# Masking unchosen experts behind the relu on VectorE, not in PSUM, in a GNN and mixture-of-experts kernel

## The chip, the cores and the metric

The kernel runs on one core of one Trainium2 chip. The metric is the time of one execution on the device in microseconds, the median of several runs.

The core's engines run at the same time, each through its own instructions in order: TensorE (PE, with its weight loads shown as PEld), VectorE (DVE), ScalarE (ACT), GpSimd (POOL) and SyncE (SP), which here only issues DMAs. Each engine waits on semaphores for what others make. Matrix products accumulate in PSUM; everything else is in SBUF.

## The reference

Two layers over 6250 nodes with 256 features and 100000 edges. Each layer is a graph aggregation followed by a mixture of experts, with residual sums.

```python
x = x + gnn0(layernorm(x))      # segment_sum(w_e * (n @ Wl)[dst], src) + n @ Wr + biases
x = x + ffn0(layernorm(x))      # 8 experts, all applied, weighted by softmax
x = x + gnn1(layernorm(x))      # segment_sum(w_e * (n @ W)[src], dst) + bias
x = x + ffn1(layernorm(x))      # 32 experts, one chosen per node
```

The change touches the last line:

```python
logits = xf @ router_w.T + router_b
idx = argmax(logits, axis=-1)                             # one of 32 experts per node
h = relu(einsum('nd,ndh->nh', xf, W1[idx]) + b1[idx])     # D = 256, H = 64
out = relu(einsum('nh,nhd->nd', h, W2[idx]) + b2[idx])
```

## The kernel before, in words

The node features stay in SBUF as `X`, 49 tiles of 128 nodes. The kernel first sorts the edges by source for layer 0 (to about 400 us), then runs layer 0 (to about 1845 us), then layer 1.

**Layer 1's aggregation.** The edges lie in columns of 128, sorted by target. For each column POOL issues an indirect DMA that gathers 128 rows of `h1` into a tile `g` (L201, with 24 buffers), ACT multiplies by the edge weight (L230), DVE computes the rounding rest of that product (L231, a scalar_tensor_tensor with two SBUF inputs), and both halves make one tile `m` (12 buffers). DVE also makes one-hot matrices `s` of the targets, three columns at a time (L222). PE multiplies `s` and `m` into `acc` (L277). Eight columns later `acc` is copied and summed (L250, L251, L255, L262), transposed (L209), multiplied by the layer's weight (L214) and added to `X` (L215). The first 64 columns are gathered in layer 0 already ("early columns"; `early_columns` prepares their indices and weights).

**Layer 1's experts.** The nodes go in 13 blocks: 3 tiles, then 11 blocks of 4, then 2. `begin1` normalizes a block (L329 to L346, transposes at L340), computes the router's logits (L956), finds the expert of each node, makes a one-hot of it, repeated four times to fill 128 columns, and transposes this (L972) into `hotT`, which has expert numbers on partitions. It also makes `cold`, which is 1 where `hotT` is 0. All 32 experts are applied to all nodes: the hidden layer has 32 x 64 units, in 16 chunks of 128, two experts a chunk. `hidden1` makes one chunk for a block: two products with W1 (L983), a third product of `sel` and `cold` (L986), which adds -2^127 to the units of the experts that weren't chosen, and a relu with bias on ACT (L988), which turns these into 0. `outs1` multiplies the chunk by W2 and accumulates in `py` (L999); with the first chunk it also adds the chosen bias (L997). `end1` adds relu(py) to `X` (L1006) and writes it out. `sel` is made once, by DVE, at L1024, from an iota made at L119.

**The order.** The products of chunk c+1's hidden layer are written ahead of chunk c's `outs1`. Between them come columns of the next block's aggregation, spread by a plan (`aheads`, `Stream.upto`): in a block of four tiles, 64 columns over 32 places. `begin1` of the next block is called 5 chunks ahead of the end of a block. Each engine's instructions are put in order by the framework when the kernel is built; the order written is a priority, and the engine order can differ from it.

PSUM tiles that matter: `ph` has three buffers; `tr`, with one buffer, is shared by the transposes, the logits and `pg`.

Of the kernel before, what the change touches and what calls it, by code (L numbers as in the profile page):

```python
# [8 lines left out]
F32 = mybir.dt.float32  # L9
F32R = mybir.dt.float32r  # L10
BF = mybir.dt.bfloat16
I32 = mybir.dt.int32
AF = mybir.ActivationFunctionType
OP = mybir.AluOpType
AX = mybir.AxisListType

P = 128
# [5 lines left out]
NB = 4  # L23
# [11 lines left out]
NX1 = 32  # L35
H1 = 64
# [2 lines left out]
SJ = 3  # L39
LAG = 10  # L40
EARLY = 2
FAR = -2.0 ** 127
SRC_PAD = 8191
NEAR = 576
LN_EPS = 1e-5
# [4 lines left out]
def gnn_ffn_kernel(ctx: ExitStack, tc: tile.TileContext, a, out):  # L50
# [32 lines left out]
    nc = tc.nc  # L83

    const = ctx.enter_context(tc.tile_pool(name="const", bufs=1))
# [5 lines left out]
    h1 = dram.tile([NT * P, D], F32, name="h1")  # L91

    def across(name, pool=const):
# [14 lines left out]
    src_c = const.tile([P, NCOL], I32, name="src_c")  # L108
    val_c = const.tile([P, NCOL], F32, name="val_c")
# [5 lines left out]
    good1 = const.tile([P, 1], F32, name="good1")  # L115
    off = const.tile([P, 1], F32, name="off")

    which_x = const.tile([P, NX1], F32, name="which_x")
    nc.gpsimd.iota(which_x, pattern=[[1, NX1]], base=0, channel_multiplier=-1, allow_small_or_imprecise_dtypes=True)  # L119
    order = const.tile([P, NX1], F32, name="order")  # L120
    nc.gpsimd.iota(order, pattern=[[-1, NX1]], base=NX1, channel_multiplier=0, allow_small_or_imprecise_dtypes=True)
    edges_rec, edges_val = a["edges_rec"], a["edges_val"]
# [8 lines left out]
                   allow_small_or_imprecise_dtypes=True)  # L131
# [3 lines left out]
    psum = sort_ctx.enter_context(tc.tile_pool(name="psum0", bufs=1, space=bass.MemoryType.PSUM))  # L135
# [260 lines left out]
    def check_edges():  # L396
# [24 lines left out]
        for i in range(2):  # L421
# [9 lines left out]
                   allow_small_or_imprecise_dtypes=True)  # L431
    which_q = early.tile([P, P, 4], BF, name="which_q")
    nc.gpsimd.iota(which_q, pattern=[[1, P], [0, 4]], base=0, channel_multiplier=0,
                   allow_small_or_imprecise_dtypes=True)
# [3 lines left out]
                   allow_small_or_imprecise_dtypes=True)  # L438
# [180 lines left out]
    psum = dense_ctx.enter_context(tc.tile_pool(name="psum1", bufs=1, space=bass.MemoryType.PSUM))  # L619
# [12 lines left out]
    LIM = late[0] * P  # L632
    NE = EARLY * GC

    with tc.tile_pool(name="layer0", bufs=1) as wp, tc.tile_pool(name="outs0", bufs=1, side="right") as wo_pool, \
# [56 lines left out]
        def aggregate0():  # L692
            for b, tiles in enumerate(blocks0):
                idx, dl, w = edges[b]
                for i, t in enumerate(tiles):
                    acc = psum.tile([P, 2, D], F32, tag="agg", name="acc", bufs=2)
                    for j in range(EW):
                        if j % SJ == 0:
                            s = one_hots(wp, dl[:, i, :], j, 3)
                        m = weighted(wp, h0, idx[:, i, j:j + 1], w[:, i, j:j + 1], 12, 6)  # L700
                        nc.tensor.matmul(acc, s[:, j % SJ, :], m, start=(j == 0), stop=(j == EW - 1))  # L701
                        if j == EW - 1:
                            for half in range(2):
                                nc.vector.tensor_add(X[:, t, :], X[:, t, :], acc[:, half, :])
                        yield

            for _ in columns1(wp, psum, range(NE), h1[:LIM, :], idx_e, w_e, (3, 12, 6, 2)):
                yield
            while True:
                yield  # L710
# [84 lines left out]
        def load1(k, half):  # L795
# [4 lines left out]
            else:  # L800
                cs = slice(half * NC1 // 2, (half + 1) * NC1 // 2)
                x = a["L1_ffn_W2"].rearrange("e h d -> (e h) d").rearrange("(c p) d -> p c d", p=P)
                nc.sync.dma_start(w2f[:, cs, :], x[:, cs, :])


        idx_e = wp.tile([P, NE], I32, name="idx_e")
        w_e = wp.tile([P, NE], F32, name="w_e")

        def early_columns():
            nc.vector.tensor_scalar(w_e, src_c[:, :NE], float(LIM), None, op0=OP.is_lt)  # L810
            nc.vector.tensor_tensor(w_e, w_e, val_c[:, :NE], OP.mult)
            nc.vector.tensor_scalar(idx_e, src_c[:, :NE], float(LIM - 1), None, op0=OP.min)


        n_late = len(late)
# [74 lines left out]
        block = begin0(blocks0[0])  # L890
# [47 lines left out]

    with tc.tile_pool(name="layer1", bufs=1, reuse_waits="tile") as wp, \
            tc.tile_pool(name="psum_y1", bufs=1, space=bass.MemoryType.PSUM, reuse_waits="tile") as psum_y:  # L940

        sel_x = wp.tile([P, NX1, H1], BF, name="sel")
        sel = sel_x.rearrange("q (c s) i -> q c (s i)", s=2)
        nought = wp.tile([P, 2 * D], BF, name="nought")

        done = []
# [1 line left out]
        def begin1(pool, tiles):  # L948

            n = len(tiles)  # L950
            nw = n * P
            nT = norm_t(pool, psum, tiles)
            pl = psum.tile([P, NB, NX1], F32, tag="tr", name="pl", bufs=1)
            for j in range(n):
                for k in range(2):
                    nc.tensor.matmul(pl[:, j, :], nT[:, k, j * P:(j + 1) * P], rw[:, k, :],  # L956
                                     start=(k == 0), stop=(k == 1))
            hot = work.tile([P, NB, NX1], F32, tag="hot", name="hot")
            top = work.tile([P, NB], F32, tag="top", name="top")
            g, m = hot[:, :n, :], top[:, :n]  # L960
            nc.vector.tensor_tensor(g, pl[:, :n, :], br1[:, None, :].to_broadcast([P, n, NX1]), OP.add)
            nc.vector.tensor_reduce(m, g, AX.X, OP.max)
            nc.vector.tensor_tensor(g, g, m[:, :, None].to_broadcast([P, n, NX1]), OP.is_equal)

            nc.vector.tensor_tensor(g, g, order[:, None, :].to_broadcast([P, n, NX1]), OP.mult)
            nc.vector.tensor_reduce(m, g, AX.X, OP.max)
            nc.vector.tensor_tensor(g, g, m[:, :, None].to_broadcast([P, n, NX1]), OP.is_equal)
            hots = work.tile([P, NB, P // NX1, NX1], F32, tag="hots", name="hots", bufs=1)
            nc.scalar.activation(hots[:, :n], g[:, :, None, :].to_broadcast([P, n, P // NX1, NX1]), AF.Copy)
            pg = psum.tile([P, NB * P], F32, tag="tr", name="pg", bufs=1)  # L970
            for j in range(n):
                turned = nc.tensor.transpose(pg[:, j * P:(j + 1) * P], hots[:, j], ident)  # L972
            hotT = pool.tile([P, NB * P], BF, tag="hotT", name="hotT", bufs=2)
            done[:] = [turned, nc.scalar.activation(hotT[:, :nw], pg[:, :nw], AF.Copy)]
            cold = pool.tile([P, NB * P], BF, tag="cold", name="cold", bufs=2)
            done.append(nc.vector.tensor_scalar(cold[:, :nw], pg[:, :nw], 0.5, None, op0=OP.is_lt))
            return nT, hotT, cold, nw

        def hidden1(pool, block, c):
            nT, _, cold, nw = block  # L980
            ph = psum.tile([P, NB * P], F32, tag="mm", name="ph", bufs=3)
            for k in range(2):
                nc.tensor.matmul(ph[:, :nw], w1f[:, k, c * P:(c + 1) * P], nT[:, k, :nw],  # L983
                                 start=(k == 0), stop=False)

            nc.tensor.matmul(ph[:, :nw], sel[:, c, :], cold[:, :nw], start=False, stop=True)  # L986
            hm = pool.tile([P, NB * P], F32, tag="hm", name="hm", bufs=4)
            nc.scalar.activation(hm[:, :nw], ph[:, :nw], AF.Relu, bias=b1[:, c:c + 1])  # L988
            return hm

        def outs1(block, c, now, py, n):
# [22 lines left out]
        with tc.tile_pool(name="flow1", bufs=1, reuse_waits="tile") as flow:  # L1014

            sums = Stream(columns1(flow, psum, range(NE, NREAL), h1, src_c, val_c, (5, EW + 6, 12, 4)))
            cum = [0] + [min(CS * (2 * tiles[-1] + 2) + CS // 2, NREAL) + LAG - NE for tiles in blocks1[1:]]
            plans = aheads(cum, 2 * NC1, [4] + [8] * (len(blocks1) - 1))
            block = begin1(flow, blocks1[0])

            behind = ExitStack()
            for ins in done:
                behind.enter_context(tc.issue_after(ins.ins))
            nc.vector.tensor_scalar(sel_x, which_x[:, :, None].to_broadcast([P, NX1, H1]), 0.0, FAR,  # L1024
                                    op0=OP.is_equal, op1=OP.mult)
            nc.vector.memset(nought, 0.0)
            hm = hidden1(flow, block, 0)
            for b, tiles in enumerate(blocks1):
                n = len(tiles)
                last = b + 1 == len(blocks1)  # L1030
                py = psum_y.tile([P, NB, D], F32, tag="y", name="py", bufs=1)
                mine = block
                for c in range(NC1):
                    sums.upto(plans[b][2 * c])
                    now = hm
                    if c + 1 < NC1:
                        hm = hidden1(flow, block, c + 1)
                    elif not last:
                        block = after
                        hm = hidden1(flow, block, 0)  # L1040
                    sums.upto(plans[b][2 * c + 1])
                    if b == 0 and c == 3:
                        behind.close()
                    outs1(mine, c, now, py, n)

                    if c == NC1 - (3 if b == 0 else 5) and not last:
                        after = begin1(flow, blocks1[b + 1])
                end1(flow, tiles, py)
# [60 lines left out]
```

## Time and profile before

| What | Value |
|---|---|
| Median of 3 runs | 2913.34 us (2908.56 to 2917.24) |
| The profiled execution's own time | 2906.32 us |
| Its span, first to last instruction | 2904.5 us |
| Mean granted TensorE clock | 0.974 |
| Busy over the span: PE, PEld | 2685.0 us (92%), 1750.0 us (60%) |
| Busy over the span: DVE, ACT, POOL | 2017.1 (69%), 1626.5 (56%), 1921.2 us (66%) |
| First chunk of layer 1's experts, last gather, last product | about 1860, 2784.5, 2897 us |
| Third products of `hidden1` (L986), one for a full block of 4 tiles | 208; record of 0.38 us |

Durations are of one execution, 7.0 us below the median. The records of PE's products overlap, since they are pipelined: the time from one start to the next is what a product costs. A few records of products are missing. In a line of a group, the figures after the first bar are busy time and the mean of one in ns, after the second the idle time just before and what ended most of it. In a line of the timeline the first two figures are start and duration in us.

### The profile page before, as it was taken

Reading aid. Unit: us, or ns where it says so; the run is one execution under the profiler, and the core shown is the slowest. Engines: PE = TensorE matmul, PEld = TensorE weight load, DVE = VectorE, ACT = ScalarE, POOL = GpSimd, SP = SyncE. Lnnn points to the kernel's source line nnn. Section 1 sums busy time; section 2 is a strip of 40 time slices with the busy share of each in tenths; the row PEclk is TensorE's granted clock in tenths of the full one; section 3 lists DMA queues with packets and bytes.
Section 4 is the critical chain, followed back from the end, with each engine's and each line's share of the span. In section 5 each row is a group of like instructions: output and inputs, shape, how many; then the busy total and the mean of one; then the engine's idle time right before and its main releaser. Section 6 shows DMA issues by size and latency. Waiting matters only on the chain.

```text
span 2904.5 us, 36970 instructions
## 1 busy us (share of the span) xinstructions
PE 2685.0 (92%) x10276; PEld 1750.0 (60%) x10336; DVE 2017.1 (69%) x4917; ACT 1626.5 (56%) x3790; POOL 1921.2 (66%) x1932
## 2 busy tenths in 40 slices
PE   5888848889999999999999998779999999999998
PEld 2444427666566666666666665556666666666666
DVE  8999978788767767667666646566666666666630
ACT  6777837655555555555555545355555555555532
POOL 4666667777767666776675527577777777777720
PEclk9999969999999999999999998989999999999999
DMA  4000043333333333333332214333333333333310
GB/s 150 19 19 19 19 144 97 104 101 101 93 99 96 89 102 93 91 103 95 90 100 82 82 40 126 95 108 100 108 109 109 106 108 102 108 107 109 109 46 12
DMA packets 123140, 260.73 MB, mean 90 GB/s; under 512 B 32236, under 2 KB 68904, under 8 KB 122920
## 3 DMA queue, kind: packets, MB, share of 16 engines
q0 software_dynamic: 79872, 218.21, 26.5%
q1 hardware_dynamic: 31672, 32.42, 3.4%
q10 hardware_dynamic: 11376, 7.60, 0.8%
q8 instruction: 85, 1.39, 0.2%
q14 instruction: 135, 1.11, 0.1%
HBM read 238.87 MB, written 19.25 MB: 89 GB/s over the span
## 4 chain that ended last, share of the span: by engine, by line
PE 60%; DMA 10%; issue 6%; DVE 5%; ACT 3%; POOL 2%; another core or an unknown queue 0%; ACTq 0%; POOLq 0%; SPq 0%; DVEq 0%
PE ph L748 19%; PE py L760 10%; PE py L999 8%; PE ph L983 8%; PE acc L701 6%; DMA g<-h,src_c 5%; PE acc L277 4%; DMA g<-h,idx 3%; POOL g L201 2%; DVE m L231 2%; ACT m L230 2%; DMA g<-h,idx_e 1%; PE ph L214 1%; PE tr L340 1%; PE pl L720 1%
## 5 line engine op out<-in xcount | busy, mean ns | idle before, releaser
L201 POOL DMA_INDIRECT g<-h,idx x882 | 900.0, 1020 | 390.7 <-DVE m L231 171.5
L201 POOL DMA_INDIRECT g<-h,src_c x718 | 724.9, 1010 | 244.2 <-issue 110.8
L230 ACT ACTIVATE m<-g,w 128x256 fp32r<-128x256 f32 x882 | 393.9, 500 | 254.5 <-PE acc L701 130.7
L230 ACT ACTIVATE m<-g,val_c 128x256 fp32r<-128x256 f32 x718 | 349.8, 503 | 278.5 <-PE acc L277 133.2
L751 ACT ACTIVATE hT<-ph,shift,scale 128x512 f32<-128x512 f32 (+3 forms) x480 | 328.8, 696 | 313.4 <-PE ph L748 312.0
L231 DVE SCALAR_TENSOR_TENSOR m<-g,val_c,m 128x256 fp32r<-128x256 f32 x718 | 336.8, 482 | 213.0 <-ACT m L230 209.2
L231 DVE SCALAR_TENSOR_TENSOR m<-g,w,m 128x256 fp32r<-128x256 f32 x882 | 397.3, 476 | 44.4 <-ACT m L230 43.5
L748 PE MATMUL ph<-nT,w 128*128 128x512 f32 (+3 forms) x960 | 376.1, 527 | 25.0 <-ACT hT L751 24.9
L760 PE MATMUL py<-wo,hT 128*128 128x256 f32 x1568 | 379.7, 385 | 14.0 <-DVE X L762 11.4
L999 PE MATMUL py<-w,hm 128*128 128x256 f32 x1568 | 385.2, 384 | 2.0 <-ACT hm L988 1.9
L983 PE MATMUL ph<-nT,w 128*128 128x512 f32 (+2 forms) x832 | 377.2, 574 | 0.0
L701 PE MATMUL acc<-m,s 128*128 128x512 f32 x882 | 339.7, 488 | 37.1 <-DVE scale L657 24.7
L748 PE MATMUL ph<-hT,w 128*128 128x512 f32 (+3 forms) x960 | 369.9, 519 | 0.5 <-ACT hT L751 0.5
L760 PEld LDWEIGHTS py<-wo,hT 128*128 128x128 f32 x1568 | 293.2, 192 | 80.6 <-DVE X L762 28.0
L277 PE MATMUL acc<-m,s 128*128 128x512 f32 x782 | 335.4, 502 | 5.7 <-DVE m L231 5.4
L999 PEld LDWEIGHTS py<-w,hm 128*128 128x128 f32 x1568 | 290.9, 192 | 51.8 <-ACT hm L988 3.9
L222 DVE TENSOR_TENSOR s<-col,dl 128x384 fp32r<-128x384 f32 x294 | 161.3, 550 | 185.7 <-PE acc L701 183.5
L748 PEld LDWEIGHTS ph<-nT,w 128*128 128x128 f32 x960 | 176.9, 197 | 175.1 <-issue 119.6
L748 PEld LDWEIGHTS ph<-hT,w 128*128 128x128 f32 x960 | 175.7, 193 | 118.5 <-issue 89.1
L988 ACT ACTIVATE hm<-ph,b 128x512 f32<-128x512 f32 (+2 forms) x208 | 136.8, 659 | 194.7 <-PE ph L986 141.9
L701 PEld LDWEIGHTS acc<-m,s 128*128 128x128 f32 x882 | 169.2, 195 | 108.9 <-issue 50.1
L983 PEld LDWEIGHTS ph<-nT,w 128*128 128x128 f32 x832 | 158.0, 192 | 102.2 <-issue 81.8
(248 smaller groups left out, 3343.7 us busy)
## 6 DMA issues: line engine op xcount, KB each, us to landing
g<-h,idx POOLq DMA_INDIRECT x882, 2.8
g<-h,src_c POOLq DMA_INDIRECT x718, 2.8
h<-hs SPq DMA_DIRECT2D x25, 256.0 KB, 2.1
X<-in_x_dram SPq DMA_DIRECT2D x12, 512.0 KB, 9.4
out_dram<-o SPq DMA_DIRECT2D x11, 512.0 KB, 3.4
h<-hs SPq DMA_DIRECT2D x9, 512.0 KB, 3.1
w<-in_L_ffn_W_dram ACTq DMA_DIRECT2D x2, 2048.0 KB, 11.9
wo<-in_L_ffn_Wo_dram ACTq DMA_DIRECT2D x1, 2048.0 KB, 21.1
```

The lines of the kernel that those rows point to most:

```text
L201: nc.gpsimd.indirect_dma_start(out=g, out_offset=None, in_=h, in_offset=bass.IndirectOffsetOnAxis(ap=idx, axis=0))
L222: nc.vector.tensor_tensor(s[:, :n], col[:, None, :].to_broadcast([P, n, P]), dl[:, j:j + n, None].to_broadcast([P, n, P]), OP.is_equal)
L230: nc.scalar.activation(m[:, 0, :], g, AF.Copy, scale=w)
L231: nc.vector.scalar_tensor_tensor(m[:, 1, :], g, w, m[:, 0, :], op0=OP.mult, op1=OP.subtract)
L277: nc.tensor.matmul(acc, s[:, (j - js.start) % SJ, :], m, start=opens, stop=done)
L701: nc.tensor.matmul(acc, s[:, j % SJ, :], m, start=(j == 0), stop=(j == EW - 1))
L748: nc.tensor.matmul(ph[:, :nw], (w1, w2)[layer][:, e, k, m * P:(m + 1) * P], src[:, k, :nw], start=(k == 0), stop=(k == 1))
L751: nc.scalar.activation(hT[:, m, :nw], ph[:, :nw], AF.Relu, bias=shift[:, layer, c:c + 1], scale=scale[:, layer, c:c + 1])
L760: nc.tensor.matmul(py, hT[:, k, j * P:(j + 1) * P], wo[:, e, k, :], start=(k == 0), stop=(k == 1))
L983: nc.tensor.matmul(ph[:, :nw], w1f[:, k, c * P:(c + 1) * P], nT[:, k, :nw], start=(k == 0), stop=False)
L988: nc.scalar.activation(hm[:, :nw], ph[:, :nw], AF.Relu, bias=b1[:, c:c + 1])
L999: nc.tensor.matmul(py[:, j, :], now[:, cols], w2f[:, c, :], start=False, stop=(c == NC1 - 1), skip_group_check=True)
```

## The change

The third product of `hidden1` goes. Instead `begin1` makes, for each block, a tile `whose` on all 128 partitions. A product of a constant `to_expert` with `hotT` gives the number of each node's expert, less 1 in the upper half of the partitions (whose units are those of odd experts), and DVE copies this to bf16. Behind each relu, DVE compares `whose` with 2c and multiplies the chunk by the result, in place (`hm`, f32). So chunk c keeps a unit only where the node's expert is the unit's. `cold`, `sel` and the iota behind `sel` go. `to_expert` is made by POOL at the start (a memset and an iota). `early_columns` writes in place into `src_c` and `val_c` where it had its own tiles, with two DVE instructions where there were three.

```diff
@@ constants
-    which_x = const.tile([P, NX1], F32, name="which_x")
-    nc.gpsimd.iota(which_x, pattern=[[1, NX1]], base=0, channel_multiplier=-1, allow_small_or_imprecise_dtypes=True)
+    to_expert = const.tile([P, P], BF, name="to_expert")
+    nc.gpsimd.memset(to_expert, 0.0)
+    nc.gpsimd.iota(to_expert[:NX1, :].rearrange("q (s i) -> q s i", s=2), pattern=[[-1, 2], [0, H1]], base=0,
+                   channel_multiplier=1, allow_small_or_imprecise_dtypes=True)
@@ aggregate0
-            for _ in columns1(wp, psum, range(NE), h1[:LIM, :], idx_e, w_e, (3, 12, 6, 2)):
+            for _ in columns1(wp, psum, range(NE), h1[:LIM, :], src_c, val_c, (3, 12, 6, 2)):
@@ early_columns
-            nc.vector.tensor_scalar(w_e, src_c[:, :NE], float(LIM), None, op0=OP.is_lt)
-            nc.vector.tensor_tensor(w_e, w_e, val_c[:, :NE], OP.mult)
-            nc.vector.tensor_scalar(idx_e, src_c[:, :NE], float(LIM - 1), None, op0=OP.min)
+            nc.vector.scalar_tensor_tensor(val_c[:, :NE], src_c[:, :NE], float(LIM), val_c[:, :NE],
+                                           op0=OP.is_lt, op1=OP.mult)
+            nc.vector.tensor_scalar(src_c[:, :NE], src_c[:, :NE], float(LIM - 1), None, op0=OP.min)
@@ begin1
-            cold = pool.tile([P, NB * P], BF, tag="cold", name="cold", bufs=2)
-            done.append(nc.vector.tensor_scalar(cold[:, :nw], pg[:, :nw], 0.5, None, op0=OP.is_lt))
-            return nT, hotT, cold, nw
+            pe = psum.tile([P, NB * P], F32, tag="tr", name="pe", bufs=1)
+            nc.tensor.matmul(pe[:, :nw], to_expert, hotT[:, :nw], start=True, stop=True)
+            whose = pool.tile([P, NB * P], BF, tag="whose", name="whose", bufs=2)
+            done.append(nc.vector.tensor_copy(whose[:, :nw], pe[:, :nw]))
+            return nT, hotT, whose, nw
@@ hidden1
                 nc.tensor.matmul(ph[:, :nw], w1f[:, k, c * P:(c + 1) * P], nT[:, k, :nw],
-                                 start=(k == 0), stop=False)
-            nc.tensor.matmul(ph[:, :nw], sel[:, c, :], cold[:, :nw], start=False, stop=True)
+                                 start=(k == 0), stop=(k == 1))
             hm = pool.tile([P, NB * P], F32, tag="hm", name="hm", bufs=4)
             nc.scalar.activation(hm[:, :nw], ph[:, :nw], AF.Relu, bias=b1[:, c:c + 1])
+            nc.vector.scalar_tensor_tensor(hm[:, :nw], whose[:, :nw], 2.0 * c, hm[:, :nw],
+                                           op0=OP.is_equal, op1=OP.mult)
@@ layer 1
-        sel_x = wp.tile([P, NX1, H1], BF, name="sel")
-        sel = sel_x.rearrange("q (c s) i -> q c (s i)", s=2)
...
-            nc.vector.tensor_scalar(sel_x, which_x[:, :, None].to_broadcast([P, NX1, H1]), 0.0, FAR,
-                                    op0=OP.is_equal, op1=OP.mult)
```

More of the change, by code (lines that the diff above doesn't have):

```diff
@@ L41 @@
 EARLY = 2
-FAR = -2.0 ** 127
 SRC_PAD = 8191
@@ L803, in load1 @@
                 nc.sync.dma_start(w2f[:, cs, :], x[:, cs, :])
-        idx_e = wp.tile([P, NE], I32, name="idx_e")
-        w_e = wp.tile([P, NE], F32, name="w_e")
         def early_columns():
-            nc.vector.tensor_scalar(w_e, src_c[:, :NE], float(LIM), None, op0=OP.is_lt)
-            nc.vector.tensor_tensor(w_e, w_e, val_c[:, :NE], OP.mult)
-            nc.vector.tensor_scalar(idx_e, src_c[:, :NE], float(LIM - 1), None, op0=OP.min)
+            nc.vector.scalar_tensor_tensor(val_c[:, :NE], src_c[:, :NE], float(LIM), val_c[:, :NE],
+                                           op0=OP.is_lt, op1=OP.mult)
+            nc.vector.tensor_scalar(src_c[:, :NE], src_c[:, :NE], float(LIM - 1), None, op0=OP.min)
         n_late = len(late)
@@ L974, in begin1 @@
             done[:] = [turned, nc.scalar.activation(hotT[:, :nw], pg[:, :nw], AF.Copy)]
-            cold = pool.tile([P, NB * P], BF, tag="cold", name="cold", bufs=2)
-            done.append(nc.vector.tensor_scalar(cold[:, :nw], pg[:, :nw], 0.5, None, op0=OP.is_lt))
-            return nT, hotT, cold, nw
+            pe = psum.tile([P, NB * P], F32, tag="tr", name="pe", bufs=1)
[3 more added lines that the diff above has]
+            return nT, hotT, whose, nw
         def hidden1(pool, block, c):
-            nT, _, cold, nw = block
+            nT, _, whose, nw = block
             ph = psum.tile([P, NB * P], F32, tag="mm", name="ph", bufs=3)
```

## Prediction

> **What bounds the kernel now.** I read the page first, then busy times by stretch, then the timeline of POOL beside that of DVE, then the waits. The change sits in layer 1, from about 1860 us to the end. On the page:
>
> ```profile
> L201 POOL DMA_INDIRECT g<-h,src_c x718 | 724.9, 1010 | 244.2 <-issue 110.8
> L231 DVE SCALAR_TENSOR_TENSOR m<-g,val_c,m 128x256 fp32r<-128x256 f32 x718 | 336.8, 482 | 213.0 <-ACT m L230 209.2
> L988 ACT ACTIVATE hm<-ph,b 128x512 f32<-128x512 f32 (+2 forms) x208 | 136.8, 659 | 194.7 <-PE ph L986 141.9
> ```
>
> Busy time by stretch (length; PE, PEld, DVE, ACT, POOL):
>
> ```profile
> 1860.00:2785.00 925.00, 887.00 (x3462) 610.33 (x3515) 596.92 (x1430) 495.88 (x1083) 710.54 (x705) 0.99 0.36 106
> 2785.00:2905.00 120.00, 111.22 (x469) 79.67 (x474) 17.24 (x49) 27.98 (x55) 0.41 (x1) 0.98 0.04 14
> ```
>
> PE at 96% and POOL at 77% invite the reading that PE is the bound. The timeline of POOL (start, duration, idle before) corrects it:
>
> ```profile
> 2466.27 1.02 POOL L201 DMA_INDIRECT g<-h,src_c  x1 [0.30 <-issue]
> 2467.60 1.31 POOL L201 DMA_INDIRECT g<-h,src_c  x1 [0.30 <-issue]
> 2469.22 0.95 POOL L201 DMA_INDIRECT g<-h,src_c  x1 [0.30 <-DMA g<-h,src_c]
> ```
>
> The 0.30 us ahead of each gather is always 0.30, whatever releaser is named: it is POOL's own gap. The 692 gathers from 1870 to 2780 us start 1.315 us apart in the mean, 1.245 at least: 1.25 of their own and 65 ns of lengthening (45 us in all). POOL never waits for a buffer; it paces the stage until its last gather at 2784.5. PE is only just behind: a block of four tiles takes 84 us, 64 gathers x 1.31, and PE's own start-to-start times add up to 80.8. The rest shows here (us, times, longest), 2140 to 2726:
>
> ```profile
> ACT m L230 <- PE acc L277: 99.0, 93, 2.6
> ACT m L230 <- DMA g<-h,src_c: 42.5, 70, 1.3
> PE tr L340 <- DVE xn L346: 10.7, 6, 2.6
> ```
>
> ACT runs ahead and waits sometimes for PE to free an m, sometimes for a gather's landing. DVE executes in order behind gathered data, so `begin1`'s statistics come late and PE stops at its transposes, some 1.7 us a block. After 2785 there are no gathers; PE alone sets the end.
>
> The lengthening has a cause that the trace shows. DVE, same moments:
>
> ```profile
> 2467.53 0.56 DVE L222 TENSOR_TENSOR s<-col,dl_c 128x384 fp32r<-128x384 f32 x1 [0.39 <-PE acc L277]
> 2469.25 0.41 DVE L255 TENSOR_TENSOR sums<-sums 64x256 f32<-64x256 f32 x1
> ```
>
> The one-hot, with two SBUF inputs, starts before the gather of 2467.60 and ends 0.49 us into it; that gather takes 1.31 instead of 0.95. L255 starts just after the next gather's start, which stays at 0.95. Over all 692 the rule holds: a two-SBUF-input DVE instruction already running at a gather's start lengthens it by (its remaining time - 115 ns); any other leaves it at 0.945. L231 costs 26.7 us so (38 ns each), L222 13.7 (59 ns each).
>
> [...] in the trace a cold product at 2859.78 is followed by py at 2860.00, 0.22.
>
> **The change, part by part.**
>
> *PE, removed.* 208 cold products: 176 x 0.216 + 16 x 0.16 (three tiles) + 16 x 0.11 (two tiles) = 42.3 us. Added: 13 products `pe`, 2.7 us. Before 2785 this buys almost nothing, since POOL's gathers cover it; if that cover went, it would be 39.6 us. Only the tail counts: 4.4 chunks of block 10 x 0.216, 16 of block 11 x 0.216 and 16 of block 12 x 0.107 = 6.1 us. A PE that isn't the limit may also stand up to a chunk (4.8 us) further ahead at the last gather; 0 to 5, I take 2.
>
> *DVE, added.* A mask behind each relu, 128x512, f32 and bf16 in, both SBUF, immediate scalar. No row shows it[...]. DVE goes from 597 to about 722 of 925 us, 78%: not the bound. `whose` replaces `cold` at the same size (0.69 from PSUM), `sel`'s 1.41 us go.
>
> *What queues behind the mask.* DVE waits there for the relu, and behind stand L231, L222, the sums and `begin1`'s statistics. PE waits for those; but from 2100 us its aggregation product starts 11 us or more, in 99 cases of 100, after the DVE product it needs, and the gathers have 24 buffers at 1.3 us each. The statistics come up to 0.7 us later, and PE stops longer at its transposes: hidden by POOL's pace, 0 to 2 us, I take 0. `hm` is needed two products later (3.4 us on, 1.7 for two tiles), relu plus mask take 1.4 and 0.9: no stall, except for the last chunk, where PE already waits 0.16 us for the relu. There 0.45 us are added.
>
> *POOL, lengthened.* The mask has two SBUF inputs. At a random moment an instruction of d ns costs the gathers (d-145)^2/(2 x 1310): for L231 43 (seen 38), for L222 64 (seen 59), for a mask 113, with three tiles 65. Under the gathers lie 16 of three tiles, 144 + 12 of four: 18.6 us. But the moments needn't be random. When ACT waits for landings, its relu comes right behind an m (2440.02, then 2440.43), so a mask would run about 2441.1 to 2441.8, between the gathers of 2440.9 and 2442.2, and cost nothing. So 0 to 18.6; I take half, 9. For the same reason L231 hits less: while ACT was under 3 us behind its gather (195 gathers) the lengthening was 45 ns, at 3 to 6 us (356) 64 to 76. With PE lighter the first kind should grow from 28% to some 60%: about -9 ns x 692 = -6 us; bounds -14 and +5 (masks push products into starts). POOL ends 3 us later.
>
> *At nothing.* `to_expert`'s memset and iota: POOL then waits 9.4 us for a bias; without that cover 0.4. `early_columns` in place: 0.2 us of DVE fewer, at 393 us. `pe` waits for hotT: up to 0.7 a block, under POOL's pace; 0.5 in all in the tail. The slot `tr` is held longer by it, same cover. `sel` gone at 1856: POOL's stream is running since 1845, nothing gained. No DMA moves, and the queue of SP stays as it is.
>
> Sum: POOL +3, tail -6.1 + 0.45 + 0.5, PE's lead -2: **-4 us**. The profiled execution took 2906.3 (span 2904.5), 7.0 below the median of 2913.3; it would go to 2902, the median to **2909**. A measurement tells about 0.3% (8.7 us) from no change, so this is no change; its own range is 2905 to 2922.
>
> **The rivals.**
>
> *Masks hit at random (slower).* All 18.6 us, products pushed into starts +5, tail -5: +18, 2931. For it: DVE at 78% runs more in bursts, and the stretches where ACT lags show 64 to 76 ns. Against: a lighter PE puts ACT on the gathers' beat. It decides from 21 ns more per gather, 14 us, at which the tail no longer brings the sum under +0.3%.
>
> *Gathers on beat (faster).* 45 ns each instead of 65: -14; masks +3; tail -5 and lead -2: -18, 2895. For it: the stretches at 45 ns. Against: L222 waits for PE and keeps its 14 us.
>
> *PE is the bound (faster).* All 39.6 us of products go: 2874. For it the 96%. Against: no gather waits, and 1.25 us is their least; this needs most of the 45 us of lengthening to vanish as well.
>
> *The mask doesn't spare the product.* Excluded by the diff: `stop` moves to the second k and the product is gone.
>
> **How the numbers follow.** No change 0.38, masks at random 0.24, on beat 0.32, PE bound 0.06: faster 0.38, same 0.38, slower 0.24. From 2888 to 2931 leaves out the PE-bound case and about half of the slower one, under 2 in 10.
>
> **What would show it.** After the change: L986 gone, 208 masks at 0.69; gather spacing 1.315 within 0.02; last gather within 2775 to 2805; from it to the end 112 to 115 us instead of 120; PE waiting longer at L340. Gathers with gaps other than 0.30, or PE still without stalls at L340, would prove the reading of POOL wrong; a spacing over 1.335 the slower rival right, under 1.30 the faster one.

## The result, and the profile after

The kernel became slower: 2922.85 us against 2911.34 us, medians of 11 runs each, a ratio of 1.0037 [1.0028, 1.0046]. That is +11.5 us where -4 was forecast. It lies inside the widest stated range, 2888 to 2931 us, but above the 2905 to 2922 that was given to no change, and on the side to which I had given the smallest chance.

The two profiled executions (spans 2904.5 and 2918.5 us) can be cut at the same three points, read from the starts of the gathers and of the last `py` product:

| us | before | after | difference |
|---|---|---|---|
| First gather of layer 1's main stream | 1840.95 | 1841.54 | +0.6 |
| From it to the last gather | 943.51 | 963.20 | +19.7 |
| From the last gather to the last product | 112.32 | 105.76 | -6.6 |
| From the last product to the end | 7.77 | 8.00 | +0.2 |

So the tail gained what it should, and the gather stage lost three times as much. The groups of both kernels between 1846 us and the end of the gathers, with before's line first (after the first bar: busy us and the mean of one in ns):

```profile
L201 POOL DMA_INDIRECT g<-h,src_c x711 | 718.2, 1010 | 216.6 <-issue 108.5 <-DVE m L231 50.3 <-DVE s L222 17.1
```

```profile
L202 POOL DMA_INDIRECT g<-h,src_c x711 | 736.2, 1035 | 219.0 <-issue 79.1 <-DVE m L232 53.3 <-DMA g<-h,src_c 22.5
```

There are as many gathers with the same idle time ahead of them (0.30 us each), but each takes 25 ns more. The page of after counts 782 gathers in this group, because the 64 early ones now read `src_c` too; hence the comparison by window.

Busy time by stretch of the kernel after (length; PE, PEld, DVE, ACT, POOL):

```profile
1861.00:2805.00 944.00, 873.92 (x3360) 605.53 (x3359) 686.73 (x1607) 503.22 (x1088) 729.52 (x705) 0.97 0.35 104
2805.00:2919.00 114.00, 105.71 (x441) 77.54 (x439) 35.23 (x82) 27.68 (x54) 0.73 (x1) 0.97 0.05 15
```

PE fell from 96% to 93% of the first stretch, DVE stands at 73%, and the stretch is 19 us longer: no engine is full. The mask itself costs DVE what was forecast (tile `whose`; min/median/max in ns):

```profile
L986 DVE SCALAR_TENSOR_TENSOR hm<-whose,hm x208: 424/684/762, 1861.2 to 2909.3; 128x512 f32<-128x512 bf16 x88, 128x384 f32<-128x384 bf16 x8, 128x256 f32<-128x256 bf16 x8
```

The waits of 2140 to 2726 us (us, times, longest):

```profile
ACT m L231 <- DMA g<-h,src_c: 85.1, 128, 3.1
ACT m L231 <- PE acc L278: 72.4, 73, 2.0
PE tr L341 <- DVE xn L347: 26.4, 7, 5.0
```

ACT now waits for landings 128 times instead of 70, and PE stops at its transposes for 26.4 us instead of 10.7. That the gathers are slower isn't the reason: e3 and e4 below, whose gathers keep the pace of before, show the like (123 and 92 waits; 19.0 and 21.7 us). But ACT came much less close to the gathers than forecast. The part of the gathers whose product on ACT starts less than 3 us after the gather does grew from 30% (207 of 692) to 34% (237 of 694), where the forecast went from 28% to some 60%.

**How a mask lengthens one gather.** POOL, then DVE, in the kernel after (start, duration). The 0.945 us of an undisturbed gather and the 0.115 are those of the prediction's rule:

```profile
1988.00 1.28 POOL L202 DMA_INDIRECT g<-h,src_c  x1 [0.30 <-ACT sums L251]
```

```profile
1987.78 0.68 DVE L986 SCALAR_TENSOR_TENSOR hm<-whose,hm 128x512 f32<-128x512 bf16 x1
1988.38 0.41 DVE L216 TENSOR_TENSOR X<-X,ph 128x256 f32<-128x256 f32 x1
```

The mask is running when the gather starts, and ends 0.46 us into it. Less 0.115 that makes 0.345; the gather takes 1.28 where 0.945 is its own, 0.335 more. L216 follows at once, but one of its inputs is in PSUM, and it adds nothing.

**How it lengthens one that an add holds.** The same two views, elsewhere:

```profile
2368.86 2.27 POOL L202 DMA_INDIRECT g<-h,src_c  x1 [0.30 <-issue]
```

```profile
2368.83 0.41 DVE L256 TENSOR_TENSOR sums<-sums 64x256 f32<-64x256 f32 x1
2369.17 0.54 DVE L223 TENSOR_TENSOR s<-col,dl_c 128x384 fp32r<-128x384 f32 x1
2369.64 0.67 DVE L986 SCALAR_TENSOR_TENSOR hm<-whose,hm 128x512 f32<-128x512 bf16 x1
2370.24 0.40 DVE L216 TENSOR_TENSOR X<-X,ph 128x256 f32<-128x256 f32 x1
```

The add over 64 partitions ends at 2369.24. By the prediction's rule the gather would have been 0.27 us longer; it is 1.33 longer, which is the time to the end of the mask at 2370.31, less 0.115. So it was held through three instructions that followed each other without a gap; such an unbroken run is called a held run below. Of the gathers of this kernel that started in a two-input instruction with another right behind it, those in such an add were held in 12 cases of 13, those in any other in 1 of 160.

Summed over the stage, each gather's time over 0.945 us put down to the instruction, or the unbroken run of them, that was on DVE when it started:

| Lengthening of the gathers, us | before | after |
|---|---|---|
| Masks (L986 of after) alone | - | 17.2 (64 gathers) |
| A 64-partition add, held until a mask's end | - | 10.1 (11 gathers) |
| Rounding rest `m` (L231, L232 of after) | 21.3 | 15.6 |
| One-hot `s` (L222, L223 of after) | 13.3 | 15.1 |
| 64-partition adds alone | 2.7 | 1.3 |
| Other held runs | 6.1 | 1.2 |
| All of it, small ones included | 46.2 | 64.9 |

Of before's 6.1 us, 3.65 fall to one gather that was held from a one-hot to the end of the ninth instruction behind it, at 1882.37, less 0.115:

```profile
1878.60 4.59 POOL L201 DMA_INDIRECT g<-h,src_c  x1 [0.30 <-issue]
```

```profile
1878.12 0.54 DVE L222 TENSOR_TENSOR s<-col,dl_c 128x384 fp32r<-128x384 f32 x1
1881.90 0.47 DVE L231 SCALAR_TENSOR_TENSOR m<-g,val_c,m 128x256 fp32r<-128x256 f32 x1
```

### The profile page after: what moved, and what is told of

It reads as the page before. It is cut to its first block, busy times and chain, and to the rows that moved or that the text cites. A ratio compares the mean times of both kernels' runs of the same rounds, so it can differ in the third digit from the quotient of the medians.

```text
span 2918.5 us, 36818 instructions
## 1 busy us (share of the span) xinstructions
PE 2661.7 (91%) x10141; PEld 1741.3 (60%) x10141; DVE 2120.5 (73%) x5123; ACT 1633.6 (56%) x3790; POOL 1942.1 (67%) x1933
## 4 chain that ended last, share of the span: by engine, by line
PE 63%; DVE 14%; DMA 10%; issue 5%; ACT 5%; POOL 1%; ACTq 0%; POOLq 0%; DVEq 0%
PE ph L749 19%; PE py L761 10%; PE py L998 8%; PE ph L981 7%; DMA g<-h,src_c 7%; PE acc L702 5%; PE acc L278 4%; PE put L531 3%; DMA g<-h,idx 3%; DVE m L232 3%; ACT m L231 2%; DVE loads L528 1%; POOL g L202 1%; ACT loads L503 1%; PE ph L571 1%
## 5 line engine op out<-in xcount | busy, mean ns | idle before, releaser
L202 POOL DMA_INDIRECT g<-h,src_c x782 | 810.1, 1036 | 309.7 <-issue 91.2
L231 ACT ACTIVATE m<-g,val_c 128x256 fp32r<-128x256 f32 x782 | 381.7, 504 | 342.6 <-DMA g<-h,src_c 186.8
L231 ACT ACTIVATE m<-g,w 128x256 fp32r<-128x256 f32 x882 | 394.7, 500 | 258.1 <-PE acc L702 138.7
L232 DVE SCALAR_TENSOR_TENSOR m<-g,val_c,m 128x256 fp32r<-128x256 f32 x782 | 362.1, 480 | 156.6 <-ACT m L231 154.2
L232 DVE SCALAR_TENSOR_TENSOR m<-g,w,m 128x256 fp32r<-128x256 f32 x882 | 397.7, 476 | 42.9 <-ACT m L231 41.4
L998 PE MATMUL py<-w,hm 128*128 128x256 f32 x1568 | 394.4, 389 | 9.1 <-DVE hm L986 9.0
L761 PE MATMUL py<-wo,hT 128*128 128x256 f32 x1568 | 381.1, 386 | 17.2 <-DVE X L763 14.5
L278 PE MATMUL acc<-m,s 128*128 128x512 f32 x782 | 375.1, 550 | 8.6 <-DVE m L232 8.3
L702 PE MATMUL acc<-m,s 128*128 128x512 f32 x882 | 341.3, 490 | 36.8 <-DVE scale L658 24.6
L998 PEld LDWEIGHTS py<-w,hm 128*128 128x128 f32 x1568 | 297.1, 196 | 64.0 <-DVE hm L986 13.8
L223 DVE TENSOR_TENSOR s<-col,dl 128x384 fp32r<-128x384 f32 x294 | 161.4, 551 | 186.7 <-PE acc L702 184.5
```

Source lines behind the costliest of these rows:

```text
L202: nc.gpsimd.indirect_dma_start(out=g, out_offset=None, in_=h, in_offset=bass.IndirectOffsetOnAxis(ap=idx, axis=0))
L223: nc.vector.tensor_tensor(s[:, :n], col[:, None, :].to_broadcast([P, n, P]), dl[:, j:j + n, None].to_broadcast([P, n, P]), OP.is_equal)
L231: nc.scalar.activation(m[:, 0, :], g, AF.Copy, scale=w)
L232: nc.vector.scalar_tensor_tensor(m[:, 1, :], g, w, m[:, 0, :], op0=OP.mult, op1=OP.subtract)
L278: nc.tensor.matmul(acc, s[:, (j - js.start) % SJ, :], m, start=opens, stop=done)
L761: nc.tensor.matmul(py, hT[:, k, j * P:(j + 1) * P], wo[:, e, k, :], start=(k == 0), stop=(k == 1))
```

## Experiments

Theory: POOL's gathers pace the stage; the masks lengthen them because both of a mask's inputs are in SBUF, and because runs that begin with a 64-partition add and end in a mask hold them longer. Rivals: DVE is simply too busy, so that what queues behind a mask comes late (any operation of that length would do); or the loss lies in the other edits of the change. The expectations call the theory that of the port and the first rival that of the queue; the port is only a name there, no run shows one.

**A neutral operation of the mask's size in the kernel before**, once with both inputs in SBUF, once with one of them in PSUM. The product on PE stays in both.

```diff
             nc.scalar.activation(hm[:, :nw], ph[:, :nw], AF.Relu, bias=b1[:, c:c + 1])
+            # e1
+            nc.vector.scalar_tensor_tensor(hm[:, :nw], cold[:, :nw], 2.0, hm[:, :nw],
+                                           op0=OP.is_lt, op1=OP.mult)
+            # e2, in its place
+            nc.vector.scalar_tensor_tensor(hm[:, :nw], ph[:, :nw], 0.0, hm[:, :nw],
+                                           op0=OP.mult, op1=OP.max)
```

> The kernel before, with its third product kept, and behind each relu a DVE instruction of the mask's size and place with two SBUF inputs (cold < 2, times hm: it multiplies by 1). Port theory[...]: gather spacing goes from 1.315 to about 1.340 us, last gather some 18 us later, the part after the last gather as before plus 0.5: +18 us, 1.006 of before. Queue theory (the mask hurts as one more instruction in DVE's order that waits for the relu, so that products and statistics come late and PE stands): a similar rise here, +10 to +18 us, so this run alone doesn't tell; its pair with one PSUM input does.

> As the run with two SBUF inputs, but the added DVE instruction reads ph from PSUM and hm from SBUF (max of ph times 0 and hm: it leaves hm as it is), same size, same place, same wait for the relu. Port theory: spacing stays at 1.315 within 0.005, time within 3 us of before (0.999 to 1.001). Queue theory: the same rise as with two SBUF inputs, +10 us or more.

Measured: 1.0055 [1.0039, 1.0070] with two SBUF inputs, 0.9974 [0.9963, 0.9984] with one in PSUM (before: 2911.32 us). The added operations, by tile, e1 first; some records are missing:

```profile
L989 DVE SCALAR_TENSOR_TENSOR hm<-cold,hm x202: 424/688/768, 1859.9 to 2899.2; 128x512 f32<-128x512 bf16 x88, 128x384 f32<-128x384 bf16 x8, 128x256 f32<-128x256 bf16 x5
```

```profile
L989 DVE SCALAR_TENSOR_TENSOR hm<-ph,hm x208: 424/690/693, 1865.2 to 2895.4; 128x512 f32<-128x512 f32 x88, 128x384 f32<-128x384 f32 x8, 128x256 f32<-128x256 f32 x8
```

They take the same time on DVE, 0.688 and 0.690 us, at the same place. Groups of the gathers in a window of the same length, again e1 first:

```profile
L201 POOL DMA_INDIRECT g<-h,src_c x698 | 721.6, 1034 | 212.7 <-issue 82.0 <-DVE m L231 58.5 <-DVE s L222 15.2
```

```profile
L201 POOL DMA_INDIRECT g<-h,src_c x714 | 717.0, 1004 | 241.7 <-issue 89.8 <-DVE m L231 64.0 <-PE corr L878 23.3
```

1034 ns against 1004 ns for a gather, and 16 gathers fewer in the same 934 us. In e2 not one gather's lengthening falls to the added operation; in e1 16.6 us fall to it alone and 5.5 to held runs that end in it. So DVE's added time costs nothing at this place, and the second SBUF input makes the whole difference of 20.7 us between the two: the first rival doesn't explain the loss. By which mechanism the second input does it, no run shows. That e2 comes out even a little faster than before was not expected; the table at the end of this section shows where that lies.

**The kernel after with the mask replaced by e2's operation, and without it.** Both leave the masking out.

```diff
-            nc.vector.scalar_tensor_tensor(hm[:, :nw], whose[:, :nw], 2.0 * c, hm[:, :nw],
-                                           op0=OP.is_equal, op1=OP.mult)
+            # e3; e4 has nothing here
+            nc.vector.scalar_tensor_tensor(hm[:, :nw], ph[:, :nw], 0.0, hm[:, :nw],
+                                           op0=OP.mult, op1=OP.max)
```

> The changed kernel with the mask replaced by the DVE instruction that reads ph from PSUM and hm from SBUF and leaves hm as it is: the masking is left out, the DVE work, its place and its waits stay. Port theory: spacing 1.31 us, the part after the last gather 105.8 instead of 112.3 us, so 6 to 9 us faster than before: 0.997 to 0.998. Queue theory: as the changed kernel, 1.003 to 1.004.

> The changed kernel with the mask left out and nothing in its place (units of unchosen experts stay). Port theory: 0.997 to 0.998 of before, as with the PSUM input, spacing at or a little under 1.31. Queue theory: clearly faster than the run with the PSUM input, by 5 us or more. A theory that pe, whose or the changed order of the rest cost the time: still slower than before.

Measured: 0.9982 [0.9974, 0.9990] and 0.9949 [0.9937, 0.9961]. Without the mask the kernel is 12.8 us faster than before in the medians, so the other edits together lose nothing and the second rival is out. The gathers of e3 in their stage:

```profile
L202 POOL DMA_INDIRECT g<-h,src_c x709 | 718.2, 1013 | 216.8 <-issue 73.6 <-DVE m L232 61.5 <-DVE s L223 18.6
```

1013 ns where after has 1035. But the medians of e3 and e4 differ by 7.8 us. That is more than the theory of the port has room for, and it is the sign that was set for the queue (5 us or more). So the two pairs don't agree on what an operation with a PSUM input costs: -6.4 us in e2 against before, +7.8 in e3 against e4. The profiles put e3's part into the gathers (48.8 and 41.6 us of lengthening), by instructions that both kernels have. Whether the added operation moved these instructions onto the gathers, or the order of the program did, is open. The loss of the kernel after is larger: it stands 16.5 us above e3, which has the same DVE time.

**Masks in two halves; full-partition adds; masks only where there are no gathers.** Three kernels and a control.

```diff
@@ e5, e5b: after
-            nc.vector.scalar_tensor_tensor(hm[:, :nw], whose[:, :nw], 2.0 * c, hm[:, :nw],
-                                           op0=OP.is_equal, op1=OP.mult)
+            for at in (slice(0, nw // 2), slice(nw // 2, nw)):
+                nc.vector.scalar_tensor_tensor(hm[:, at], whose[:, at], 2.0 * c, hm[:, at],
+                                               op0=OP.is_equal, op1=OP.mult)
@@ e7, e7b: after; e8, e8b: before
-                nc.vector.tensor_add(s[low], s[low], halves[q - 1][low])
+                nc.vector.tensor_add(s, s, halves[q - 1])
...
-                nc.vector.tensor_add(halves[q - 1][high], halves[q - 1][high], s[high])
+                nc.vector.tensor_add(halves[q - 1], halves[q - 1], s)
@@ e6, e6b: before, its product kept for blocks 0 to 10; in 11 and 12 the mask; the change's other edits as in after
+BARE = NT - 6
...
+            if tiles[0] >= BARE:
...
+                return nT, hotT, whose, nw, True
```

> The changed kernel with each mask cut into two instructions of half the length (256 columns, about 0.42 us each, 1.3 times the DVE time of one of 0.69). Port theory, with each instruction costing the gathers (d-145)^2/(2 x 1310) ns: 2 x 28 to 29 = 57 ns a mask in place of 113, so the masks' own 17 us fall to about 9 us, and the last gather comes 6 to 10 us earlier than in the changed kernel: 0.9995 to 1.0015 of before. Queue theory or a theory of DVE's total work: 21 us more of DVE work and 416 instructions in place of 208 make it slower than the changed kernel, 1.004 or more.

> The kernel before for blocks 0 to 10, with sel, cold and the third product; blocks 11 and 12, which run when all gathers are done, take whose and the mask. Port theory: no mask lies under a gather, the part after the last gather falls from 112.3 to about 107.5 us: 4 to 5 us faster than before, 0.998 to 0.999, and faster than the changed kernel by 14 us or more. A theory that pe, whose or the mask are dear by themselves (in the tail too): 1.000 or more.

> The changed kernel with the two adds of 64 partitions (of the halves of a tile's sums) made over all 128 partitions; the sums that leave it aren't the reference's. In the trace of the changed kernel 11 gathers that met such an add were held until the end of the mask behind it, 10 us in all, while gathers that met other two-input instructions were held for that one alone. If an add of half the partitions[...]: those cases go, the lengthening falls from 65 to 55 to 58 us, 0.997 of the changed kernel, 1.000 to 1.002 of before. If it is their place in the order (back-to-back instructions that wait for nothing): the held cases stay, and so does the time, 1.003 to 1.004.

> The kernel before with the same two adds over 128 partitions (the sums aren't the reference's): the control. In its trace 2 gathers were held beyond an add, 2.4 us in all. Either theory: within 3 us of before, 0.999 to 1.001.

This first set told nothing on the question. The kernel before itself took 3281.98 us there, and its gathers no longer follow at 0.30 us. A line of POOL's timeline in e8:

```profile
2611.09 0.95 POOL L201 DMA_INDIRECT g<-h,src_c  x1 [3.58 <-DVE m L231]
```

POOL stood idle 150 to 202 us beyond its own gaps between the 718 gathers of the stage in these four (before, in its usual run: 4 us), so that its gathers were not the pace. The stage also began late there, at 2007 to 2031 us instead of 1841. The ratios were 0.9948 [0.9931, 0.9965] for e5, 0.9979 [0.9954, 1.0004] for e6, 0.9965 [0.9947, 0.9982] for e7 and 1.0000 [0.9970, 1.0029] for e8: there the mask in halves and with full adds came out ahead of the kernel before. This would fit a stage in which PE's spared time counts, but the kernel after itself has no run there. Why all was slower is open; in these four profiles no gather shows when it landed. The four were repeated later, on a chip of the same number (13, both times), and there before took 2909.48 us.

> e5 again on a usual chip: masks in two halves. Port theory: 0.9995 to 1.0015 of before, the masks' own lengthening 17 us down to about 9. Theory of DVE's total work or of its queue: 1.004 or more.

Measured: 1.0025 [1.0016, 1.0034], a little above the expected. A half takes 0.417 us, so DVE works 0.15 us more for each chunk, 1.22 times a whole mask:

```profile
L987 DVE SCALAR_TENSOR_TENSOR hm<-whose,hm x416: 281/417/496, 1861.3 to 2906.6; 128x256 f32<-128x256 bf16 x117, 128x192 f32<-128x192 bf16 x11, 128x128 f32<-128x128 bf16 x11
```

The masks' own lengthening fell from 17.2 to 8.7 us: more DVE time, half of that loss. In the time of the whole the gain is not clear: the interval touches that of the kernel after, 1.0028 to 1.0046. What didn't fall enough is the held part: 4.8 us still go to gathers that an add holds through both halves, and further runs, whose start is neither a mask nor an add over 64 partitions, hold more than in after (6 that start in an `m`).

> e7 again on a usual chip: the changed kernel with the two half-partition adds made over all 128 partitions (its sums aren't the reference's). If the half-partition add[...]: lengthening 55 to 58 us instead of 65, 1.000 to 1.002 of before. If it is their place in the order: 1.003 to 1.004.

> e8 again on a usual chip, the control: the kernel before with the two adds over 128 partitions (its sums aren't the reference's). Either theory: 0.999 to 1.001 of before.

Measured: 1.0012 [1.0004, 1.0020] for after with full adds, 0.9984 [0.9974, 0.9995] for the control. In e7b no gather is held through a run. The same moment as above, POOL and then DVE:

```profile
2367.27 1.19 POOL L202 DMA_INDIRECT g<-h,src_c  x1 [0.30 <-issue]
2368.76 0.94 POOL L202 DMA_INDIRECT g<-h,src_c  x1 [0.30 <-DVE hm L986]
```

```profile
2367.22 0.42 DVE L256 TENSOR_TENSOR sums<-sums 128x256 f32<-128x256 f32 x1
2367.55 0.55 DVE L223 TENSOR_TENSOR s<-col,dl_c 128x384 fp32r<-128x384 f32 x1
2368.02 0.68 DVE L986 SCALAR_TENSOR_TENSOR hm<-whose,hm 128x512 f32<-128x512 bf16 x1
```

Again a gather starts just after the add, and the same three follow without a gap. But it is 0.245 us longer, the add's remaining 0.37 less 0.115, and lets the rest go by. In all 13 gathers of e7b started in an add with another two-input instruction right behind, and none was held. The masks alone lengthen by 14.2 us instead of 17.2, and the whole is 53.7 us instead of 64.9. The control's is 50.9 in its profiled execution, no less than before's 46.2: before has few such runs to lose. But its median came out 2.8 us lower where no change was expected, so of the 7.5 us between after and e7b some 5 are left to the held runs by the medians. That they are gone is shown by the trace.

> The same kernel as e6 again, for a chip on which the kernel before takes its usual 2911 us (e6 met a chip where it took 3282, with POOL idle for 238 us between gathers, so that nothing was paced by the gathers). Mask in the tail alone: 4 to 5 us faster than before, 0.998 to 0.999, gather spacing as before, 1.31 us, the part after the last gather about 107.5 us. If pe, whose or the mask are dear by themselves: 1.000 or more.

Measured: 0.9985 [0.9976, 0.9993], 2903.91 us. Busy by stretch:

```profile
2784.00:2899.00 115.00, 106.60 (x442) 77.82 (x444) 34.41 (x81) 28.02 (x55) 0.28 (x1) 0.98 0.04 14
```

Its last gather starts at 2783.33 (before: 2784.46), and from there to the last product it takes 107.6 us instead of 112.3. It keeps most of the tail's gain without the stage's loss and is the version that beats both kernels here, by 0.15% over before. That is no more than the control e8b gained, so its place in the tail is shown by its trace rather than by the median.

**All runs in one table**, one profiled execution each (us; the difference of medians is to before in the same set):

| Kernel | First to last gather | Lengthening in it | Difference of the two | Last gather to last product | Median, difference |
|---|---|---|---|---|---|
| before | 943.5 | 46.2 | 897.3 | 112.3 | 0 |
| after | 963.2 | 64.9 | 898.3 | 105.8 | +11.5 |
| e1, two SBUF inputs added | 960.5 | 63.2 | 897.3 | 111.2 | +14.3 |
| e2, PSUM input added | 940.0 | 42.9 | 897.1 | 111.2 | -6.4 |
| e3, after with PSUM input | 945.6 | 48.8 | 896.8 | 105.7 | -5.0 |
| e4, after without mask | 938.4 | 41.6 | 896.8 | 106.2 | -12.8 |
| e5b, after in halves | 957.2 | 60.4 | 896.8 | 107.1 | +8.2 |
| e7b, after with full adds | 950.6 | 53.7 | 896.9 | 107.8 | +4.0 |
| e8b, before with full adds | 948.1 | 50.9 | 897.2 | 112.0 | -2.8 |
| e6b, masks in the tail only | 942.7 | 46.6 | 896.1 | 107.6 | -5.6 |

The fourth column is 896.1 to 898.3 in all ten: POOL's gaps don't grow, and whatever PE, DVE and ACT have to do, the stage is the gathers' own time plus their lengthening. With the last-but-one column this gives the differences of the medians within 2 us, e8b excepted, whose profiled execution took 6.1 us more than its median. It leaves out where the stage begins, between 1839.8 and 1845.4 us in these executions. What the table leaves open is the lengthening of the kernels that have no masks under the gathers: 41.6 to 50.9 us, by the same instructions at other moments. In several of them one early gather alone, at 1876 to 1881 us, takes part of it by a held run: 3.65 us in before and in e4, 4.5 in e6b. This scatter between programs, of up to 0.3%, is as large as e2's and e8b's gains and the difference of e3 and e4; none of those is explained. The 60.4 to 64.9 us of e5b, e1 and after lie outside it, the 53.7 of e7b only just.

## Why the prediction was wrong

- **What bounds the kernel** was right: the gaps stayed at 0.30, POOL paces the stage, and PE's 39.6 us of products there bought nothing. (The prediction's 0.216 us a product is the 0.22 of before's trace, from a third product's start at 2859.78 to the next product's; with two tiles it is 0.11, from 2866.25 to 2866.36. The 0.16 with three is an estimate between these.) The rival with PE as the bound is dead: e4, with all the products gone and no mask, gains 12.8 us and not 39.6.
- **The tail** was right: -6.1, -2 and +0.95 make -7.1; measured -6.4 with the end (the -2 for PE's lead wasn't measured apart). In the last chunk PE waited 0.16 us for the relu before and now 0.56 for the mask, +0.40 for the priced 0.45:

```profile
2908.76 0.47 ACT L984 ACTIVATE hm<-ph,b 128x256 f32<-128x256 f32 x1 [1.25 <-PE ph L981]
2909.26 0.43 DVE L986 SCALAR_TENSOR_TENSOR hm<-whose,hm 128x256 f32<-128x256 bf16 x1 [1.30 <-ACT hm L984]
2909.74 0.73 PEld L998 LDWEIGHTS py<-w,hm 128*128 128x128 f32 x4 [0.56 <-DVE hm L986]
```

- **The mask's price on DVE** was right: 0.684 for 0.69 us, which was the author's estimate; before's trace shows 0.690 for `cold` (L976), of the same size but with one input, from PSUM. The sum to 722 us was not: the 172 masks that it puts under the gathers make 117 us at 0.69 us and, with three tiles, at the 0.557 that L986 of after shows, 714 in all; measured 687. DVE at 73% was indeed not the bound, as e2 shows.
- **L231 hitting less**, -6, came true in size, 21.3 to 15.6 us, but by luck. Its reason was that a lighter PE lets ACT follow the gathers, and ACT's share near them grew to 34% instead of 60%. Nor does a lighter PE go with it in the runs: e1, which keeps all the products, has 15.4 us by the same count, and e4, which has none and no mask, 17.5. Without the mask's term the forecast's sum is -13, and e4 measured -12.8; with such a part in it, this agreement is luck too.
- **The step that failed** is "POOL, lengthened", and in it "So 0 to 18.6; I take half, 9". There I argued that ACT would move onto the gathers' beat and that a relu on it puts its mask between two starts. ACT hardly moved, and the masks alone lengthened 64 gathers for 17.2 us, close to the whole 18.6 worked out for random moments. That mis-sizes the sum by 8.
- **What it had no term for** is the held run. Its rule gave a lengthening by the instruction running at the start and said "any other leaves it". Eleven gathers were held to the end of a mask that wasn't yet running, +10.1 us; in e7b there are none. Before's own trace has 6.1 us of held runs, 2.4 of them begun by an add over 64 partitions, so "over all 692 the rule holds" was not so: the gather at 1878.60 breaks it. The 26.7 us that were put down to L231 seem to contain such runs, since L231's own part is 21.3 in the table above.
- **The sum again**, with the measured terms in it: masks 17.2, held 10.1, other held runs -4.9, `m` -5.7, `s` +1.8, adds alone -1.4, small ones +1.6, POOL's gaps +1.0, tail with the end -6.4 and start +0.6 give +14, as between the two profiled executions; between the medians it is +11.5.
- **The slower rival's** mechanism was the right one, masks at random moments, and so was its sign of being right, a spacing over 1.335: the gathers of after start 1.341 us apart. Its +18 was too high. Of its +5 for "products pushed into starts" only the one-hot's +1.8 came, `m` fell by 5.7, and the held runs, which it did not name, made up for part of that.

## What to carry to other kernels

In this stage, which indirect DMAs on GpSimd pace, an operation for VectorE was not priced by its time but by whether both inputs are in SBUF: the same 0.69 us, 173 times under the gathers, cost more with two inputs in SBUF than with one in PSUM: 16.5 us (after against e3) and 20.7 (e1 against e2). Without a planned phase, take its moments as random: the estimate is (d-145)^2 over twice the gathers' spacing for each, from the lengthening that before's trace shows. For the masks that gave 18.6 for 17.2 us; for `m` it gives 31 for the 21.3 of before and is too much. A clever alignment of engines that follow each other by chance is no reason to halve it. And work that PE was spared was worth something only where PE sets the end (-6.6 us in the tail, nothing under the gathers), so make such a trade only there, as e6b does; how much that gains is within the scatter here.

## What the runs showed of the hardware

- A gather that started in an add over 64 partitions with two SBUF inputs was mostly held through the two-input instructions that followed without a gap: over the eight kernels with such adds in 32 cases of 42 where one followed, in the two with 128 partitions in none of 20. Other instructions did it rarely (in after in 1 case of 160), but with some weight: in before and in e4 a run that begins with a one-hot held one gather 3.65 us longer, over ten and nine instructions. Why the gather didn't come in between them was not found.
- The loss grew with more than the length: 0.684 us of mask cost 99 ns an instruction (17.2 us over the 173 that start before the last gather), and halves of 0.417 us 25 ns each (8.7 over 346). The formula gives 111 and 28, in the same proportion.
- A gather that started just behind a two-input instruction's start, with no earlier DVE instruction still running, was seldom lengthened: up to 50 ns behind 1 of 15, at 70 to 100 ns 35 of 40 (before and after together). The formula's 145 ns fits that roughly, as the rule's 115 and some 30 more.
- With products taken from PE and masks put on DVE the stage became longer, by 19.7 us, without any engine being full: PE 93%, POOL 77% and DVE 73% busy, in a stage that POOL bounds.
